# Recurrence in groups of one, one, two, two and two sequences beside the local streams, the input in three transfers, activation tables put in after planning

## Chip, cores and metric

One core of a Trainium2 chip runs the whole program. The metric is the device time in microseconds (us) of one launch; lower is better. PE is the matrix engine, DVE the vector engine, ACT the scalar engine with its function tables, POOL the general engine, and SP a sequencer that issues transfers.

## What is computed

Eight sequences of 256 tokens with 128 channels pass through eight layers, each followed by `layernorm(x + layer(x))`. Only the first three matter here.

```python
# layer 1: a gated linear recurrence (RG-LRU)
gate_x = sigmoid(block_diag_linear(x, ig_w, ig_b))
gate_a = sigmoid(block_diag_linear(x, ag_w, ag_b))
log_a = -8.0 * gate_a * softplus(a_param)
a, a2 = exp(log_a), exp(2.0 * log_a)
normed_x = x * gate_x * sqrt(clip(1.0 - a2, 1e-07))
p = cumprod(a, axis=1)
p_prefix = clip(concatenate([ones, p[:, :-1]], axis=1), 1e-07)
h = p_prefix * cumsum(normed_x / p_prefix, axis=1)
x = layernorm(x + h)
# layer 2: two blocks of local attention (window 64, 8 heads of 64) with a GELU feed-forward net
# layer 3: a Mamba block: gates, causal convolution, 16 states per channel scanned over time
# layers 4 to 8: a mixture of 32 experts (top 1), two attention blocks with 16 heads,
# a mixture of 8 experts (top 2) with a shared expert, typed attention, a ternary linear layer
```

Each sequence is independent in the first three layers, so layer 1 of one sequence can run beside layer 2 or 3 of another.

## The kernel before

The residual stream lies by channel: 128 partitions by 2048 columns, 256 columns for a sequence (`S`). Stages are traced one after another: `rglru`, `local_mamba`, `moe1`, `chunked`, `moe2`, `typed`.

**Recurrence.** `rglru_group(b0, tiles, work)` does four sequences at once in four tiles of 128 x 1024 (`gx`, `ga`, `sh`, `pp`). Two matmuls with `wg` for each pair of sequences give the gates (tile `gate`), ACT takes the sigmoids (L1013), two Exp (L1017, L1018), a Ln and an Exp (L1025, L1026). DVE does products, the running products and sums as scans (L1021, L1033) and a reciprocal (L1028). A layernorm per sequence ends it (L893 to L918): a matmul with `centre`, Square, a matmul with `mean`, Ln, Exp, a product into `x_rglru`. `rglru` runs it for sequences 0 to 3 and lets nothing else be traced meanwhile; sequences 4 to 7 are one more group inside `local_mamba`.

**Streams.** In `local_mamba`, `interleave` traces up to four generators `one_sequence(b)` at a time, each the two local blocks of a sequence, with a lag of 24 of its units; a finished sequence goes on to `mamba_sequence`, of which two are live. The group of sequences 4 to 7 is an extra generator. A local block starts with a shift of its input (tile `h`, L1062 to L1064), then matmuls `qk` and `vps` with `w_local`, transposes `qkt`, scores `sc`, maxima `nm`, exponentials `e` on ACT (L1146), transposes `pt`, outputs `o`, and a feed-forward net with GELU (`ge`, L1194). Before the first block, `w_local` is scaled by a layernorm weight and its bias is folded through small matmuls (`b1`, L1368, L1369). A Mamba sequence hands 33 rows to DRAM (`xs`, L1254), reads them back spread over the partitions (`bc`, L1262), and scans on DVE (`hs`, L1297 to L1300).

**Order.** After all stages are traced, `_Order` plans a list schedule over the instructions, with a cost per form (`LENGTHS`: time of occupation and time to the result, ns), a price for leaving PE's or ACT's present mode (`STAY`), and an offset per tile and stage added to the traced priority (`BIAS`). `impose` then makes each engine keep that order: no instruction overtakes another on its engine, and SP issues transfers in the planned order too. A transfer on SP also waits for the one issued eight before it, whose semaphore it takes over.

**Transfers.** `x_in` is one transfer of 1 MB. Two transfers clear the DRAM buffers `places` from a zeroed tile, 1.28 MB each. `w_local` comes in two of 1.56 MB.

**Activation tables.** ACT holds one set of functions at a time; a load (ACT_TABLE_LOAD in the profile, about 1283 ns) changes it. Where a function of the wrong set follows, the compiler puts a load in. The set with both Exp and Ln is asked for by hand: `exp_ln` adds a load in the traced program at set places (after sigmoids, GELU, Silu), bound to the instruction before it by `keep`, and the planner carries these loads along as instructions of set 1. One more load, for Silu, stands at the end of `route1`.

Of the kernel before, what the change touches and what calls it, by code (L numbers as in the profile page):

```python
# [23 lines left out]
P = 128  # L24
# [285 lines left out]
class _Order:  # L310
# [12 lines left out]
    STAY = dict(PE=70, ACT=310)  # L323
    BIAS = {
        "ACT  1": 495, "ACT  3": -495, "ACT d 2": -1445, "ACT e 4": -700, "ACT e 6": 370, "ACT fh 4": -30, "ACT four 4": 630, "ACT four 5": -345,
        "ACT ge 2": 385, "ACT got 3": 50, "ACT got 5": 590, "ACT k 2": -275, "ACT kp 4": -40, "ACT lakq 2": -75, "ACT lavp 2": -95, "ACT lg 2": 620,
        "ACT lnrs 1": 225, "ACT lnrs 2": -280, "ACT lnsq 2": 40, "ACT ot 6": 75, "ACT ptsb 2": -740, "ACT qsq 2": -5, "ACT r 2": -70, "ACT rg 1": -590,
        "ACT rg 2": -320, "ACT rn 2": 55, "ACT rs 4": -50, "ACT rs 6": -25, "ACT s 6": -190, "ACT savp 2": -5, "ACT sg 3": 560, "ACT sh 5": -250,
        "ACT spl 1": -410, "ACT spt 1": -15, "ACT st 6": 460, "ACT v 2": 25, "ACT xc 2": -2725, "ACT xchunked 2": -400, "ACT xchunked 4": -390,
        "ACT xs 2": 10, "ACT xsq 4": -660, "DVE ab 4": 720, "DVE bt 3": -1225, "DVE bt 5": 190, "DVE centre 0": -205, "DVE d 2": -10,  # L330
        "DVE decaypart 4": -240, "DVE e 2": 50, "DVE four 5": 105, "DVE fs 4": 10, "DVE gate 2": -345, "DVE gate 5": -320, "DVE get 2": 180, "DVE get 4": 5,
        "DVE get 5": 850, "DVE got 4": -40, "DVE h 2": 5, "DVE h 5": -525, "DVE hs 2": 5, "DVE k 5": -680, "DVE lares 2": -200, "DVE lg 4": 665,
        "DVE nm 2": -135, "DVE nm 6": -95, "DVE oh 2": -285, "DVE oh 4": 2440, "DVE oh 5": -180, "DVE ptsb 2": 20, "DVE ptsb 6": -250, "DVE put 2": 190,
        "DVE put 4": 480, "DVE q 5": 470, "DVE q 6": 785, "DVE r 2": -120, "DVE rc 2": -270, "DVE rc 4": 175, "DVE route 2": -345, "DVE s 2": 20,
        "DVE s 5": -95, "DVE s 6": 1585, "DVE sares 2": 30, "DVE sel 4": -50, "DVE sg 3": -250, "DVE sm 4": 365, "DVE spt 1": 810, "DVE st 6": 150,
        "DVE sum 2": -705, "DVE t 5": 400, "DVE th 4": 650, "DVE u 2": 255, "DVE vec 2": 50, "DVE we 4": -30, "DVE wlocal 2": 1325, "DVE xc 2": -1830,
        "DVE xla 4": -580, "DVE xlf 4": 75, "DVE xlocal 2": -860, "DVE xmoe 6": 10, "DVE xpf 4": -10, "DVE xrglru 2": 205, "DVE xsa 4": 485, "DVE ys 3": 100,
        "DVE z 4": -190, "PE a 2": 50, "PE acc 5": 10, "PE b 2": 30, "PE bt 3": 1010, "PE bt 5": -580, "PE cum 2": 80, "PE cum 4": -1270, "PE fold 2": 105,
        "PE g 2": -700, "PE gate 1": -345, "PE gate 2": 345, "PE hps 4": -15, "PE kps 4": 95, "PE lg 2": 205, "PE lin 6": -1140, "PE ln 1": 355,
        "PE ln 2": -45, "PE o 6": -910, "PE out 4": -35, "PE pg 5": -20, "PE proj 5": 100, "PE proj 6": -570, "PE ps 4": -455, "PE pt 2": -25,  # L340
        "PE pt 4": -125, "PE pu 3": 2550, "PE pu 5": -720, "PE py 3": 740, "PE qkt 2": -1425, "PE raw 2": -1360, "PE rows 2": 585, "PE sc 2": -60,
        "PE sc 4": 30, "PE sc 6": -1215, "PE v 5": 470, "PE v 6": -20, "PE vps 2": 1025, "PE vps 4": -10, "PE wo 2": 60, "PE wo 6": -855, "PE wout 2": -95,
        "PE xps 2": -790, "PE y 2": 20, "PE z 2": 40, "PE zt 4": -20, "POOL biasrows 3": -595, "POOL e 4": 415, "POOL e 6": -305, "POOL got 5": 490,
        "POOL km 5": 665, "POOL mean 0": 635, "POOL one 0": 395, "POOL places 2": -70, "POOL places 5": -240, "POOL q 5": 50, "POOL q 6": -325,
        "POOL rest 4": -990, "POOL rg 1": -25, "POOL rows 4": 85, "POOL ss 2": -20, "POOL t 2": 595, "POOL u 2": 110, "POOL zero 0": -35,
        "POOL zeros 1": -385, "SP bc 2": 200, "SP cst 3": -455, "SP got 3": 535, "SP got 5": 505, "SP outdram 6": 275, "SP places 1": 1460,
        "SP rottable 0": 45, "SP routetables 0": 495, "SP rows 4": -370, "SP scales 2": 40, "SP vec 0": -1475, "SP wattn 2": 15, "SP wmoe 2": -150,
        "SP wmoe 4": -150, "SP wmoe 5": -100, "SP xs 2": -660,
    }
    LENGTHS = {  # L350
        "ACT  LoadActFuncSet  ": (1178, 1283), "ACT d Ln 128x512 128x512": (544, 649), "ACT da Exp 128x255 128x255": (403, 508),
        "ACT e Abs 128x256 128x256": (460, 565), "ACT e Exp 128x128 128x128": (422, 527), "ACT e Exp 128x256 128x256": (460, 565),
        "ACT e Exp 128x512 128x512": (526, 631), "ACT four Exp 128x2 128x2": (98, 203), "ACT got DMACopy 128x512 128x512": (451, 3502),
        "ACT h TensorCopy 64x255 64x255": (295, 400), "ACT k TensorCopy 128x512 128x512": (484, 589), "ACT lnrs Exp 128x256 128x256": (317, 422),
        "ACT lnsq Square 128x256 128x256": (278, 383), "ACT ot TensorCopy 128x512 128x512": (490, 595), "ACT qsq Square 128x512 128x512": (498, 603),
        "ACT r Relu 128x256 128x256": (462, 567), "ACT rg Exp 128x1020 128x1020": (1039, 1144), "ACT rg Ln 128x1024 128x1024": (949, 1054),
        "ACT rn Exp 128x16 128x16": (111, 216), "ACT rn Ln 128x16 128x16": (116, 221), "ACT rs Exp 128x2 128x2": (97, 202),
        "ACT rs Ln 128x2 128x2": (98, 203), "ACT sh Silu 128x512 128x512": (492, 597), "ACT xc Identity 128x256 128x256": (465, 570),
        "ACT xc Silu 128x512 128x512": (524, 629), "ACT xchunked TensorCopy 128x256 128x256": (260, 365), "ACT xmoe Identity 128x256 128x256": (404, 509),
        "ACT xs TensorCopy 33x256 33x256": (255, 360), "ACT xsq Square 128x128 128x128": (296, 401), "DVE biaspart TensorCopy 96x256 96x256": (198, 283),  # L360
        "DVE decay TensorScalarPtr 128x512 128x512": (516, 601), "DVE decaypart TensorCopy 128x512 128x512": (334, 419),
        "DVE four TensorScalarPtr 128x4 128x4": (74, 159), "DVE ge TensorScalarPtr 128x256 128x256": (384, 469),
        "DVE ge TensorScalarPtr 85x256 85x256": (368, 453), "DVE h TensorTensor 128x256 128x256": (317, 402),
        "DVE hs TensorScalarPtr 128x1024 128x1024": (2191, 2276), "DVE hs TensorTensor 128x1024 128x1024": (1123, 1208),
        "DVE mv BNStatsAggregate 128x2 128x6": (85, 170), "DVE nm TensorTensor 128x8 128x8": (67, 152), "DVE ptsb TensorCopy 128x512 128x512": (594, 679),
        "DVE rc Reciprocal 128x16 128x16": (158, 243), "DVE rc Reciprocal 128x4 128x4": (83, 168), "DVE rc Reciprocal 128x8 128x8": (109, 194),
        "DVE rg TensorScalarPtr 128x256 128x256": (580, 664), "DVE rottable TensorScalarPtr 128x256 128x256": (260, 345),
        "DVE s TensorScalarPtr 128x128 128x128": (253, 338), "DVE s TensorTensor 128x256 128x256": (324, 409), "DVE st BNStats 128x6 128x128": (197, 282),
        "DVE sum TensorReduce 128x32 128x448": (736, 821), "DVE t TensorScalarPtr 128x256 128x256": (385, 470),
        "DVE t TensorTensor 128x512 128x512": (595, 680), "DVE vec TensorTensor 128x1 128x1": (60, 145), "DVE vec TensorTensor 85x1 85x1": (59, 144),  # L370
        "DVE vs TensorCopy 128x512 128x512": (594, 679), "DVE wlocal TensorScalarPtr 128x682 128x682": (483, 568),
        "DVE x TensorScalarPtr 128x256 128x256": (369, 454), "DVE xc TensorScalarPtr 128x254 128x254": (384, 469),
        "DVE xla TensorScalarPtr 128x256 128x256": (429, 514), "DVE xlocal TensorTensor 128x256 128x256": (310, 395),
        "DVE xpf TensorScalarPtr 128x256 128x256": (577, 662), "DVE z TensorScalarPtr 128x128 128x128": (292, 377),
# [62 lines left out]
    def group(self, i):  # L437
# [5 lines left out]
        if e == "ACT":  # L443
            return 1 if op == "LoadActFuncSet" else self.SETS.get(str(x.func).split(".")[-1]) if op == "Activation" else None
        return None

    def change(self, i):
        x, e, op = self.ops[i]
        if e == "ACT":
            return 0.0 if op == "LoadActFuncSet" else self.TABLE  # L450
# [120 lines left out]
    def length(self, i):  # L571
# [20 lines left out]
        if e == "ACT":  # L592
            if op == "LoadActFuncSet":
                return float(self.TABLE), float(self.TABLE)
# [1805 lines left out]
```

## Time and profile before

| | us |
|---|---|
| median of 8 runs | 1673.44 |
| lowest, highest | 1671.38, 1680.12 |
| the profiled execution | 1670.69 |
| its span from first to last instruction | 1668.6 |
| busy: PE | 1429.4 (86%) |
| busy: DVE | 1138.4 (68%) |
| busy: ACT | 975.3 (58%) |
| busy: POOL | 580.1 (35%) |

The mean granted clock of PE is 0.951 of full speed. Busy shares are means over stages with different limits: which wait matters is read stage by stage. In a row of the profile, `out<-in` are the program's tile names, `xN` the count, and the bracket after a row tells how long the engine was idle before it and what ended that.

### The profile page before, as it was taken

The numbers are of one execution on the slowest core, as the hardware profiler recorded it, in microseconds if no ns is written. First come the engines' busy times: TensorE is split into PE (matmuls) and PEld (weight loads), VectorE is DVE, ScalarE is ACT, GpSimd is POOL, SyncE is SP. The second block draws the span as 40 slices with busy tenths as digits, with TensorE's granted clock in tenths as the row PEclk, the third lists the DMA queues.
The fourth block names the chain that finished last, engine by engine and source line by source line (L and its number), as shares of the span: only waits on it lengthen the run. The fifth ranks groups of instructions, "written<-read, shape, count | busy, mean of one in ns | idle before, by whom it ended". The sixth has DMA issues, their size and how long they took to land.

```text
span 1668.6 us, 28693 instructions
## 1 busy us (share of the span) xinstructions
PE 1429.4 (86%) x10858; PEld 927.3 (56%) x10858; DVE 1138.4 (68%) x2182; ACT 975.3 (58%) x2661; POOL 580.1 (35%) x535
## 2 busy tenths in 40 slices
PE   2588897989797878677579999999997999999996
PEld 1345564545454544334367777677674775566664
DVE  5754579888989898689445566565545333588885
ACT  3777887777878779545125554545443222465654
POOL 1244452626263423200421122211214005657563
PEclk7899999999999998889789999999997999999998
DMA  5000012121212112156330000000102121000000
GB/s 196 1 1 1 1 40 64 40 64 40 64 40 64 52 51 90 52 177 214 122 115 2 8 11 11 11 7 6 44 5 68 47 81 37 15 5 4 8 5 10
DMA packets 45113, 77.97 MB, mean 47 GB/s; under 512 B 5580, under 2 KB 21988, under 8 KB 43824
## 3 DMA queue, kind: packets, MB, share of 16 engines
q1 hardware_dynamic: 39648, 70.02, 13.5%
q0 software_dynamic: 3216, 5.07, 1.1%
q8 instruction: 85, 1.39, 0.3%
q10 hardware_dynamic: 2112, 1.05, 0.2%
q14 instruction: 52, 0.43, 0.1%
HBM read 66.87 MB, written 10.76 MB: 47 GB/s over the span
## 4 chain that ended last, share of the span: by engine, by line
PE 50%; DVE 24%; ACT 10%; issue 8%; POOL 5%; DMA 2%; SPq 0%; ACTq 0%; DVEq 0%; POOLq 0%
PE vps L863 7%; PE kps L863 6%; PE sc L863 5%; DVE hs L1299 4%; PE out L863 4%; DVE hs L1300 3%; PE pg L863 3%; PE pu L863 3%; PE pt L974 3%; DVE hs L1297 2%; PE o L863 2%; ACT e L1146 2%; PE py L863 2%; PE hps L863 2%; PE acc L863 1%
## 5 line engine op out<-in xcount | busy, mean ns | idle before, releaser
L863 PE MATMUL y<-hs,ident 128*128 128x512 f32 x256 | 141.3, 667 | 30.4 <-DVE hs L1300 30.3
L1151 POOL TENSOR_TENSOR e<-e,rc 128x1024 f32<-128x1024 f32 x32 | 80.5, 2516 | 227.7 <-DVE rc L1150 227.1
L1299 DVE TENSOR_TENSOR_SCAN hs<-da,hs 128x1024 f32<-128x1024 f32 x64 | 154.1, 2409 | 0.2
L2250 ACT ACTIVATE e<-sc,nm 128x128 f32<-128x128 f32 (+1 forms) x256 | 104.9, 426 | 65.7 <-DVE nm L2245 58.9
L974 PE MATMUL pt<-ident,e 128*128 128x128 f32 x768 | 118.5, 280 | 18.0 <-POOL e L1151 12.1
L1295 ACT ACTIVATE da<-d,na 128x255 f32<-128x255 f32 x256 | 110.5, 507 | 22.2 <-DVE hs L1299 19.9
L1146 ACT ACTIVATE e<-sc,nm,rn 128x128 f32<-128x128 f32 x256 | 114.6, 469 | 10.5 <-DVE nm L1141 10.0
L974 PEld LDWEIGHTS pt<-ident,e 128*128 128x128 f32 x768 | 88.1, 142 | 56.7 <-issue 20.3
L2253 POOL TENSOR_TENSOR e<-e,rc 128x1024 f32<-128x1024 f32 x48 | 91.0, 1896 | 67.1 <-DVE rc L2252 67.0
L1829 POOL TENSOR_TENSOR e<-e,rc 128x512 f32<-128x512 f32 x32 | 33.8, 1057 | 224.3 <-DVE rc L1828 195.4
L1098 POOL TENSOR_TENSOR t<-t,t 128x512 f32<-128x512 f32 x64 | 84.0, 1316 | 59.9 <-DVE t L1085 55.8
L1804 ACT COPY kp<-kps 128x512 f32<-128x512 f32 x128 | 74.7, 584 | 48.5 <-PE kps L863 47.8
L1651 POOL DMA_INDIRECT got<-ybuf,get x48 | 45.6, 951 | 159.8 <-DMA ybuf<-ys 87.6
L863 PEld LDWEIGHTS y<-hs,ident 128*128 128x128 f32 x256 | 49.0, 209 | 78.4 <-DVE hs L1300 46.2
L1297 DVE TENSOR_TENSOR hs<-u,bc 128x1024 f32<-128x1024 f32 x64 | 87.2, 1378 | 6.4 <-POOL u L1284 5.5
L1300 DVE TENSOR_TENSOR hs<-hs,bc 128x1024 f32<-128x1024 f32 x64 | 87.6, 1371 | 0.0
L976 DVE COPY ptsb<-pt 128x512 f32<-128x512 f32 x104 | 69.1, 679 | 18.1 <-PE pt L974 17.1
L863 PE MATMUL qk<-w_local,h 128*128 128x512 f32 x128 | 70.1, 635 | 13.3 <-DVE t L1085 6.4
L1840 ACT COPY vs<-vps 128x512 f32<-128x512 f32 x64 | 37.3, 584 | 67.6 <-PE vps L863 54.9
L2245 DVE TENSOR_REDUCE nm<-sc 128x4 f32<-128x1024 f32 (+1 forms) x48 | 58.3, 1215 | 16.8 <-PE sc L863 16.2
L976 ACT COPY ptsb<-pt 128x512 f32<-128x512 f32 x88 | 51.3, 583 | 31.4 <-PE pt L974 30.7
L863 PE MATMUL vps<-sa_vp,x_lf 128*32 128x512 f32 x512 | 68.5, 594 | 0.0
(380 smaller groups left out, 3777.3 us busy)
## 6 DMA issues: line engine op xcount, KB each, us to landing
bc<-xs SPq DMA_DIRECT2D x128, 256.0 KB, 4.5
w_moe<-in_e_dram SPq DMA_DIRECT2D x16, 768.0 KB, 6.3
w_attn<-in_w_dram SPq DMA_DIRECT2D x4, 1024.0 KB
w_local<-in_w_dram SPq DMA_DIRECT2D x2, 1557.0 KB
places<-zeros SPq DMA_DIRECT2D x2, 1280.0 KB, 16.9
got<-places SPq DMA_DIRECT2D x6, 256.0 KB
ybuf<-ys SPq DMA_DIRECT2D x8, 160.0 KB, 2.2
x_in<-in_x_dram SPq DMA_DIRECT2D x1, 1024.0 KB
```

The lines of the kernel that those rows point to most:

```text
L863: return self.nc.tensor.matmul(out, lhsT, rhs, start=start, stop=stop)
L974: self.last = self.nc.tensor.transpose(pt[:, j * P : (j + 1) * P], src[:, j * P : (j + 1) * P], self.ident)
L976: copy(sb.rearrange("p a b -> p (a b)"), pt)
L1098: nc.gpsimd.tensor_add(t1, t1, t2)
L1146: nc.scalar.activation(e[:, j, g, :], scs[:, j, g, :], AF.Exp, bias=nm[:, j, g : g + 1], scale=rq[:, j, g : g + 1], accum_out=sm[:, j, g : ...
L1151: nc.gpsimd.tensor_tensor(e, e, rc.unsqueeze(3).to_broadcast([P, 2, 4, P]), ALU.mult)
L1295: nc.scalar.activation(da[:, n, c, 1:S], d[:, c, 1:S], AF.Exp, scale=na[:, i : i + 1])
L1297: nc.vector.tensor_tensor(hs, u.unsqueeze(1).to_broadcast(shp), bn, ALU.mult)
L1299: nc.vector.tensor_tensor_scan(line(hs), line(da), line(hs), 0.0, ALU.mult, ALU.add)
L1300: nc.vector.tensor_tensor(hs, hs, cn, ALU.mult)
L2250: nc.scalar.activation(e[:, i, :], sc[:, i, :], AF.Exp, bias=nm[:, i : i + 1], accum_out=sm[:, i : i + 1])
L2253: nc.gpsimd.tensor_tensor(e, e, rc.unsqueeze(2).to_broadcast([P, n, keys]), ALU.mult)
```

## The change

`rglru` keeps only the softplus of `a_param` and the clears of `places`. `rglru_group` takes a number of sequences `n`. Inside `local_mamba`, groups of sequences 0, 1, and 2 with 3 use the three `da` tiles of the Mamba scan and a `bc` tile as their four buffers; the group of sequence 0 is traced at once, the rest by an extra generator `recurrences` beside the streams. Sequences 4 with 5 and 6 with 7 are two more groups in the `hs` and `bc` tiles. `one_sequence(b)` waits in tracing until its recurrence has been traced.

```diff
-        nc.sync.dma_start(self.x, ins["x"])
+        nc.sync.dma_start(self.x[:, 0:S], ins["x"][:, 0:S])
...
+        nc.sync.dma_start(self.x[:, S : 4 * S], ins["x"][:, S : 4 * S])
...
-        for l in range(2):
-            nc.sync.dma_start(self.w0[:, l, :], ins["w0"][:, l * n : (l + 1) * n])
+        nc.sync.dma_start(self.w0[:, 0, :], ins["w0"][:, 0:n])
+        nc.sync.dma_start(self.x[:, 4 * S :], ins["x"][:, 4 * S :])
+        nc.sync.dma_start(self.w0[:, 1, :], ins["w0"][:, n : 2 * n])
...
-            tiles = [w.tile([P, 4, S], F32, name=f"rg{i}") for i in range(4)]
-            for _ in self.rglru_group(0, tiles, wk):
-                pass
...
-    def rglru_group(self, b0, tiles, work):
+    def rglru_group(self, b0, n, tiles, work):
...
-        for i in range(2):
-            bs = slice(2 * i, 2 * i + 2)
+        for i in range(0, n, 2):
+            bs = slice(i, min(i + 2, n))
...
+            four = [d.rearrange("p a b s -> p (a b) s") for d in das] + [scan.tile([P, 4, S], F32, tag="bc", name="rg", bufs=3)]
+            first = [self.rglru_group(b, n, [t[:, b : b + n] for t in four], work) for b, n in ((0, 1), (1, 1), (2, 2))]
+            for _ in first[0]:
+                pass
...
+            def recurrences():
+                yield from first[1]
+                yield 4.0
+                yield from first[2]
+                for d in das:
+                    nc.gpsimd.memset(d[:, :, :, 0:1], 0.0)
+                for i, gap in ((0, 16.0), (2, 10.0)):
+                    yield gap
+                    yield from self.rglru_group(4 + i, 2, [t[:, i : i + 2] for t in tiles], work)
...
             def one_sequence(b):
+                while self.recurred <= b:
+                    yield 1.0
...
-            interleave([one_sequence(b) for b in range(B)], 4, 24.0, then, 20.0, [self.rglru_group(4, tiles, work)])
+            interleave([one_sequence(b) for b in range(B)], 4, 24.0, then, 20.0, [recurrences()])
```

All calls of `exp_ln` go, with `keep` and the Silu load of `route1`. `impose` puts the loads of the Exp and Ln set in when the order stands:

```diff
         order, _ = self.plan()
+        ring, last = [], None
+        for i in order["ACT"]:
+            g = self.groups[i]
+            if g is not None:
+                if g == 1 != last:
+                    load = self.tc.nc.scalar.preload_act_table_set("natural_log_exp_and_others")
+                    self.ops.append((load.ins, "ACT", "LoadActFuncSet"))
+                    ring.append(len(self.ops) - 1)
+                last = g
+            ring.append(i)
+        order["ACT"] = ring
```

The planner's numbers are new throughout: `STAY` goes from PE 70 and ACT 310 to PE 140 and ACT 250, all of `BIAS` is replaced, and `LENGTHS` is renewed. Some of its entries:

```diff
+        "DVE da Reciprocal 128x256 128x256": (113, 198),
+        "DVE da Reciprocal 128x512 128x512": (113, 198),
+        "DVE rg Reciprocal 128x512 128x512": (113, 198),
+        "ACT rg Exp 128x510 128x510": (361, 466),
-        "POOL got DMACopy 128x128 2560x128": (949, 2493),
+        "POOL got DMACopy 128x128 2560x128": (1280, 2500),
+        "SP xin DMACopy 128x256 128x256": (350, 1815),
```

The order imposed is therefore a new one on every engine. On SP it begins with `w1`, `wg`, the two clears of `places`, `vec`, `rot_table`, `scales`, `route_tables`, then the three parts of `x_in` and the two of `w_local`; before it began with `vec`, `x_in`, `wg`, `w_local` (both), `w1`, `rot_table`, `scales`, `route_tables`, and the clears. The compiled program has 67 table loads where it had 73.

## The prediction

> **What bounds the kernel now.** I read the page, then the chain of waits from the start, then a table by stretch of time, then the timeline around single waits. Times are us of one profiled execution, which took 1670.69 with a span of 1668.6; the median of the runs shown is 1673.44, 2.75 above it.
>
> The chain first. Its columns are start, length, what was waited for.
>
> ```profile
> 1.67 5.99 DMA wg<-in_wg_dram
> 7.79 5.56 PE gate L863 x8
> ...
> 16.55 2.44 DVE rg L1021 x4
> ...
> 22.32 6.46 DVE rg L1028
> ...
> 36.32 6.65 PE ln L863 x16
> ...
> 44.38 0.40 ACT h L1064
> ```
>
> From 1.67 to 44.38 the chain is the recurrence of sequences 0 to 3, alone: gates, scan, a 6.46 us reciprocal, layernorms. The first matmul of a local stream follows:
>
> ```profile
> 18.28 4.62 POOL L1346 TENSOR_TENSOR rot<-rot_table,scales 128x256 f32<-128x256 f32 x4 [15.04 <-DMA scales<-in_qks_dram]
> 44.65 0.67 PE L863 MATMUL qk<-w_local,h 128*128 128x512 f32 x1 [0.76 <-DVE x_rglru L918]
> ```
>
> The stretches: after the engines' busy times come the granted clock, the DMA share and GB/s.
>
> ```profile
> core 0: us, PE busy (x) PEld busy (x) DVE busy (x) ACT busy (x) POOL busy (x), PEclk, DMA share, GB/s
> 28.50:44.65 16.15, 7.57 (x26) 6.08 (x27) 8.88 (x13) 4.74 (x14) 1.30 (x9) 0.57 0.00 0
> 44.65:100.00 55.35, 38.14 (x199) 20.23 (x200) 43.58 (x69) 40.42 (x91) 19.24 (x16) 0.85 0.00 1
> 100.00:233.00 133.00, 114.72 (x831) 71.32 (x832) 70.69 (x130) 105.02 (x299) 58.63 (x68) 1.00 0.00 1
> 233.00:749.00 516.00, 421.92 (x2284) 243.39 (x2283) 453.04 (x527) 392.23 (x988) 200.17 (x170) 0.95 0.23 67
> 819.00:1668.00 849.00, 799.28 (x7281) 559.57 (x7281) 494.40 (x1348) 389.03 (x1188) 276.98 (x238) 0.97 0.09 26
> ```
>
> Before 44.65 nothing is full. From 44.65 to 100 PE is busy 69%, although streams are ready: the second group of four holds DVE and ACT there. From 100 to 233, where the first Mamba sequence hands its rows to DRAM, PE is busy 86% and DVE only 53%. From 233 to 749 DVE leads with 88%. After 819 PE has 94%.
>
> **The head: 16 us less.** In the changed program SP issues w1, wg, the two clears of `places`, vec, the rotary table, scales, route tables, then x in three parts, then w_local in two. So the first part of x, though small, stands behind 4.07 MB: w1 0.45, wg 0.13, the mask 0.14, clears 2.62, vec 0.05, tables 0.54, itself 0.13. Before, scales stood behind 5.5 MB and landed at 18.28; the GB/s by 2 us add up to 3.76 MB at 12 us and 4.56 at 14, so queue order fits within 1 us. By that curve plus 0.8: vec lands at 11.9, the first x at 13.6, the halves of w_local at 20.7 and 24.9. The issue of the first half waits for the second clear, whose bytes are through at about 11; the queue still holds tables and x then, so it does not run dry.
>
> From vec, ACT has Abs 0.2, a table load 1.28, Exp, Ln, Relu and `na` about 1.0 with DVE between, the sigmoid load 1.28: 15.7. Two sigmoids (half of 0.69 plus start, 0.45 each): 16.6. Load 1.28, decay Exp 0.5: 18.4. DVE: scan 2.44/4 = 0.61, three scalar passes 0.35, reciprocal 6.54/4 = 1.64 and start, two products 0.4, scan 0.61, product and sum 0.4: 24.0. Layernorm of one sequence (Square 0.38, Ln 0.38, Exp 0.42, product 0.42, four matmul passes of 0.63 at the cold clock): 28.0. Shift 0.4: first qk at 28.6 instead of 44.65, so 16 us. The b1 matmuls wait for the second half of w_local, 24.9, and lie under that.
>
> **What comes back: 8 us.** Three quarters of the first group's work now lies beside the streams. PE: gates 5.54 minus two half ones, 4.2, and 3/4 of 6.65, in all 9.2 at a cold clock, 5.5 at full; I take 7. ACT: 3/4 of 11.9 (four sigmoids 2.8, four Exp and Ln 4.4, twelve layernorm steps 4.7) is 8.9; smaller groups cost more starts (a 1020-wide Exp 1.15, a 255-wide one 0.51), in all some 2.1; loads ahead of the first Mamba hand-over go from 22 to 24, 2.6. DVE: 17, and about 3 for more starts; from 100 to 233 it idles 62. Up to the first xps matmul, PE has 667 matmuls instead of 661 in program order, so Mamba starts after the same work. PE bounds the rate there: 7 / 0.86 = 8. The bounds are 0 (PE idles 17 from 44.65 to 100) and 33 (second rival). DVE behind is what could be late next.
>
> **Table loads.** 73 loads become 67: two more ahead of Mamba, already counted, and eight fewer behind, 8 x 1.28 = 10.3 of ACT. Most of these were loads of two sets in a row. ACT is busy 76% from 233 to 749 but has 10% of the chain, so the gain lies between 10% of 10.3, 1, and 76%, 8; I take 3, nearer the chain. The row of a switch:
>
> ```profile
> 108.65 2.64 ACT e L1146 x12
> 111.30 1.28 ACT L1194
> 112.60 0.85 ACT ge L1194 x2
> ```
>
> No gap stands on either side: a switch costs 1.28 here. The Trainium skill (ScalarE: Activation LUTs, What ACT_TABLE_LOAD costs) adds a drain and gives about 2.66 for each switch; by that the eight would free an estimated 21 of ACT, and with the same share the gain would be 6. The row decides.
>
> The Silu load ahead of the first mixture was placed early and now stands right before the first expert's activation `sg`; ACT idled 2.15 there behind PE (826.79), so it costs nothing, and 1.28 without that cover. The three `da` memsets (0.21 together) move on POOL behind the group of sequences 2 and 3, whose tiles they clear; the first Mamba scan, some 100 us later, is the only one to wait for them: nothing.
>
> **Three transfers.** Two more issues of 0.42 on SP, behind nothing that ACT or PE await: nothing. Small pieces did not slow the queue: 407 to 410 GB/s from 18 to 22 us, with clears and tables in flight. A rule speaks against this part: the Trainium skill (DMA: Bandwidth & Descriptors, Bandwidth) says to batch DMAs to 1 MiB or more for 75% of peak. By it, with its fixed 2.0 us for each of two more transfers paid in the open, an estimate of the gain would be 4 smaller. The transfers here stand in a queue, and I leave it at the row.
>
> **Order elsewhere.** The planner's costs and offsets all change, so every engine's order does. The instructions behind 819 are the same and PE is 94% busy there; I put 0, with 6 either way.
>
> Sum: -16 + 8 - 3 = -11. Span 1657.6, profiled time 1659.7, median 1673.44 - 11 = 1662.4. I say 1662.
>
> **Rivals.**
>
> *All of it is kept.* Pieces of 1 or 2 sequences fit idle slots: PE idles 17 and ACT 15 from 44.65 to 100, and the long reciprocal there no longer stalls everyone. Then 16 for the head and 8 for the loads: -24, 1649. Against: PE is 86% busy later, so moved work must be paid somewhere.
>
> *Each group stalls the streams: slower.* From 55 to 90 PE was busy 19 of 35 us, 11 under its 86%, while one group went through ACT and DVE in fixed order. Four groups now lie beside streams; at 11 each that is 44 instead of 11, 33 more, against 16 and 3: +14, 1687. For it: the diff's costs let a 512-wide reciprocal take 0.198, while the row says 6.54/2 = 3.3, and 0.198 for 256 where it is 1.64; that is 12 us of DVE time which the fixed order does not know of, with softmax maxima queued behind. Against: by sequences, not groups, it is 11 x 7/4 = 19, only 8 more than before. It decides from 19 us of new stall.
>
> *Nothing is left.* DVE bounds from 233 on and the Mamba cadence (hand-overs 85.6, 84.5 and 84 apart at first) does not care what came earlier: the moved DVE work of 20 us then returns the head's 16, and the loads' 3: about 1673.
>
> *It does not do what it says:* were x really late, behind slower clears (their 2.62 MB take 6.7 us at 390 GB/s, 12 at the 216 of an early slice), the head gains 11, and the sum is -6: 1667. It is inside the forecast.
>
> **Chances.** Forecast, between -4 and -20: 0.60. All kept or more: 0.11. Nothing left, within 0.2% or 3.3 us, about what a measurement of this kernel can tell from no change: 0.09. Stalls: 0.20. Faster 0.71, same 0.09, slower 0.20. The range 1648 to 1678 goes from all kept to a third of the way into the stalls.
>
> **What would show it.** In the profile after: the first qk at 28 to 30; clears landing ahead of x; the first Mamba hand-over at 222 to 227; 67 loads; from 819's counterpart on, 849 plus or minus 6. Wrong would be a first qk later than 36, a hand-over later than 233, or PE under 65% between the first qk and 100 us.

## The result, and the profile after

The changed kernel took 1681.13 us (median of 15 runs, 1678.2 to 1683.76) beside 1675.43 for the kernel before (42 runs): a ratio of 1.0035, 95% interval [1.0027, 1.0044]. It is slower by about 6, where the forecast was 11 faster. The profiled execution took 1679.41 with a span of 1677.6, 9.0 above the span before. Ten of the eighteen kernels run later fell on slower occasions, on which the kernel before takes 1695 instead of 1675 (the expectations call them a slower chip, but the record gives one chip number, 6, to occasions of both kinds); ratios are always to the kernel before on the same occasion.

The chain of waits of the changed kernel from the start (start, length, what was waited for):

```profile
3.04 1.19 SPq L810
...
4.26 1.38 SPq L813
...
8.24 8.65 DMA x_in<-in_x_dram
...
16.94 2.09 PE gate L877 x4
...
22.73 1.66 DVE da L1025
...
28.11 1.36 PE b L877 x8
...
30.53 0.52 PE b L877 x4
...
31.61 1.30 PE b L877 x6
32.91 1.06 PE gate L877 x2
33.97 2.56 PE qk L877 x3
```

The recurrence of four sequences before the first local stream has become that of one: its reciprocal takes 1.66 on the chain instead of 6.46. But the chain now begins with SP: the six issues behind the two clears take 1.19 to 1.44 each, and x lands only at 16.9. Just ahead of the first qk, PE does the bias matmuls `b` and gates of the next group. The timeline of the changed kernel shows what this does to ACT and PE:

```profile
13.39 0.20 ACT L1044 ACTIVATE sp_e<-vec 128x1 f32<-128x1 f32 x1 [11.37 <-DMA vec<-in_vec_dram]
...
16.98 0.23 ACT L1345 ACTIVATE na<-vec 128x32 f32<-128x32 f32 x1 [0.98 <-DMA x_in<-in_x_dram]
17.22 1.28 ACT L1011 ACT_TABLE_LOAD   x1
18.52 0.47 ACT L1011 ACTIVATE da<-gate,vec 128x256 f32<-128x256 f32 x1
...
33.76 2.77 PE L877 MATMUL qk<-w_local,h 128*128 128x512 f32 x3
```

`na` reads only `vec`, and the table load and the sigmoids stand behind it. Its row names x, which landed at the same time, but `na` needs nothing of x; what it follows, here as in e7 below, is the end of the softplus on DVE, `c`, at 16.81:

```profile
16.67 0.14 DVE L987 TENSOR_SCALAR c<-sp_l 128x1 f32<-128x1 f32 x1
```

That softplus could start only when `vec` was there, at 13.39. The first qk came at 33.76 instead of 44.65: 10.9 of the 16 that were forecast. The stretches (columns as in the prediction: busy times, then granted clock, DMA share, GB/s):

```profile
33.76:100.00 66.24, 46.83 (x232) 25.83 (x231) 40.85 (x70) 44.26 (x114) 21.28 (x25) 0.85 0.00 1
100.00:247.40 147.40, 123.56 (x815) 74.01 (x813) 95.32 (x157) 115.14 (x309) 58.88 (x66) 0.93 0.00 1
247.40:754.50 507.10, 425.35 (x2295) 243.97 (x2294) 450.03 (x525) 379.36 (x974) 205.08 (x168) 0.95 0.23 69
821.60:1281.20 459.60, 435.95 (x4803) 319.43 (x4803) 253.75 (x797) 214.47 (x505) 97.70 (x108) 0.98 0.08 23
1281.20:1677.00 395.80, 365.24 (x2479) 241.72 (x2478) 238.34 (x552) 175.90 (x685) 179.06 (x130) 0.97 0.10 29
```

From 100 to the first Mamba hand-over PE has a granted clock of 0.93, where it had 1.00, and DVE 95 us of work where it had 71. The hand-over comes at 247.4 instead of 233.0; the eighth at 754.5 instead of 749.2; the first mixture begins at 821.6 instead of 819.4. Behind that the instructions are the same, but the stretch to the first read of `rows_chunked` takes 459.6 instead of 452.3; the rest, 396, is unchanged. So in this pair 2 of the 9 arose before the mixture and 7 behind it; in the pair of repeats below (e6, e5) it is 7 and 4.

The runs on which the rest of this text rests, by their profiles: first qk, start of the 200th and of the 1000th matmul, first Mamba hand-over, start of the first mixture, from there to the end, and the ratio from the timed runs. An asterisk marks the slower occasions.

| kernel | qk | 200th | 1000th | hand-over | mixture | to the end | ratio |
|---|---|---|---|---|---|---|---|
| before | 44.7 | 97.4 | 222.5 | 233.0 | 819.4 | 849.2 | 1 |
| before, again (e6) | 45.4 | 97.8 | 223.4 | 234.0 | 820.7 | 849.6 | |
| changed | 33.8 | 86.5 | 233.6 | 247.4 | 821.6 | 856.0 | 1.0035 |
| changed, again (e5) | 34.0 | 87.6 | 237.1 | 250.9 | 827.8 | 853.7 | 1.0026 |
| changed, again (e13) | 33.8 | 86.9 | 236.3 | 250.1 | 824.0 | 853.3 | 1.0053 |
| clears last (e4)* | 44.4 | 96.4 | 249.9 | 263.6 | 837.9 | 868.4 | 1.0091 |
| clears last, `na` free (e7) | 28.0 | 81.0 | 230.0 | 243.8 | 820.9 | 853.9 | 0.9980 |
| reciprocals on ACT (e8) | 34.2 | 85.9 | 234.9 | 248.7 | 823.6 | 853.4 | 0.9998 |
| all three (e14) | 28.0 | 77.3 | 223.5 | 237.3 | 811.0 | 847.7 | 0.9957 |
| all three (e12)* | 28.1 | 78.3 | 222.7 | 236.5 | 816.2 | 868.6 | 0.9930 |
| changed, old order behind (e1)* | 33.5 | 86.6 | 235.9 | 249.8 | 823.7 | 872.1 | 1.0002 |
| changed, old order behind (e18)* | 34.0 | 87.4 | 236.9 | 250.8 | 827.6 | 868.9 | 1.0002 |
| changed without 1 to 3 (e10)* | 33.7 | 75.4 | 233.2 | 245.2 | 820.6 | 862.7 | |
| changed without 4 to 7 (e15) | 33.9 | 87.4 | 223.4 | 235.4 | 814.0 | 853.4 | |
| before without 4 to 7 (e17)* | 44.6 | 87.4 | 215.5 | 224.3 | 810.7 | 871.2 | |

Up to the mixture one kernel agrees with itself within about 6 from run to run; so smaller differences there show nothing by themselves. At the 200th matmul the changed kernel's profiles agree within 1.1, at the 1000th within 3.5. Where the values of a run differ, its ratio is left out.

### The profile page after: what moved, and what is told of

Same layout as the page of the kernel before. It is cut to its first block, busy times and chain, and to the rows that moved or that the text cites. A ratio compares the mean times of both kernels' runs of the same rounds, so it can differ in the third digit from the quotient of the medians.

```text
span 1677.6 us, 28721 instructions
## 1 busy us (share of the span) xinstructions
PE 1447.2 (86%) x10862; PEld 935.3 (56%) x10862; DVE 1141.4 (68%) x2209; ACT 970.2 (58%) x2669; POOL 587.1 (35%) x538
## 3 DMA queue, kind: packets, MB, share of 16 engines
q1 hardware_dynamic: 39936, 70.02, 13.4%
## 4 chain that ended last, share of the span: by engine, by line
PE 53%; DVE 24%; ACT 11%; issue 6%; POOL 4%; DMA 2%; SPq 0%; ACTq 0%; DVEq 0%; POOLq 0%
PE vps L877 7%; PE sc L877 6%; PE kps L877 6%; DVE hs L1296 4%; PE out L877 4%; PE pt L974 3%; PE pg L877 3%; PE pu L877 3%; PE o L877 3%; DVE hs L1297 3%; ACT e L1144 2%; DVE hs L1294 2%; PE py L877 2%; PE y L877 2%; PE hps L877 2%
## 5 line engine op out<-in xcount | busy, mean ns | idle before, releaser
L974 PE MATMUL pt<-ident,e 128*128 128x128 f32 x768 | 114.4, 280 | 18.9 <-ACT ptsb L976 6.8
L1096 POOL TENSOR_TENSOR t<-t,t 128x512 f32<-128x512 f32 x64 | 86.9, 1358 | 73.5 <-DVE t L1083 71.3
L1657 POOL DMA_INDIRECT got<-ybuf,get x48 | 45.8, 955 | 164.7 <-DMA ybuf<-ys 87.4
L1834 POOL TENSOR_TENSOR e<-e,rc 128x512 f32<-128x512 f32 x32 | 33.7, 1054 | 196.4 <-DVE rc L1833 106.7
L976 DVE COPY ptsb<-pt 128x512 f32<-128x512 f32 x104 | 68.9, 681 | 19.9 <-PE o L877 10.9
L1297 DVE TENSOR_TENSOR hs<-hs,bc 128x1024 f32<-128x1024 f32 x64 | 82.0, 1287 | 0.0
L877 PE MATMUL vps<-sa_vp,x_lf 128*32 128x512 f32 x512 | 75.2, 594 | 0.0
L877 PE MATMUL vps<-la_vp,x_moe 128*32 128x512 f32 x512 | 70.6, 594 | 0.1
```

The costliest lines, as they stand in the source:

```text
L877: return self.nc.tensor.matmul(out, lhsT, rhs, start=start, stop=stop)
L974: self.last = self.nc.tensor.transpose(pt[:, j * P : (j + 1) * P], src[:, j * P : (j + 1) * P], self.ident)
L976: copy(sb.rearrange("p a b -> p (a b)"), pt)
L1096: nc.gpsimd.tensor_add(t1, t1, t2)
L1297: nc.vector.tensor_tensor(hs, hs, cn, ALU.mult)
```

## The experiments

The theory at first: the recurrence groups stall the streams beside them, by work that the planner took for short (S), and the order behind the mixture is worse in itself (O). The rivals: the Mamba stretch gives back what comes earlier or later (C), and the head's missing 5 are the loss (H).

**The head.** e4 changes one offset (an entry of a long line), so that the clears are issued last:

```diff
-"SP places 1": -230
+"SP places 1": 4000
```

> One offset is changed, so that SP issues the two clears of places after w_local instead of ahead of vec and x; the other engines' orders stay but for some 1 per cent of their rows. vec should land at about 4 to 5 instead of 11.9 to 13, the first x at about 7, w_local at 15 and 19, and the first qk come at 25 to 28 instead of 33.76. Theory H (the head that was forecast 5 too early is part of the loss, each us of it counts): end 6 to 8 earlier, 1673 to 1675. Theory C: the end moves by 2 at most, 1679 to 1681.

1.0091 [1.0078, 1.0104]: slower instead of faster. x was there early (its gate matmul ran at 10.85), and yet the first qk came at 44.4. The timeline of that run names the reason:

```profile
26.95 0.23 ACT L1345 ACTIVATE na<-vec 128x32 f32<-128x32 f32 x1 [18.23 <-DMA places<-zeros]
27.20 1.28 ACT L1011 ACT_TABLE_LOAD   x1
```

`na` lies in the room of `zeros`, from which the clears are written, and may not be written before they have been read; ACT works in order, so the sigmoids wait too. Neither theory had this wait. In the changed kernel itself it cost nothing: there SP issued the first half of `w_local` at 12.62, an issue that waits for the second clear, so both clears were through before `na` could start. The run still weighs the head. e1 below has the changed kernel's order up to the mixture and ran beside e4; its first qk came at 33.5 and its mixture began at 823.7. In e4 the qk came 11 later and the mixture 14 later. (The end cannot be compared in this way, because the changed kernel was not run on a slower occasion.) e7 takes the room away from `na` and keeps the clears last; PE, DVE and ACT keep the changed kernel's order to the instruction:

```diff
-            zero = w.tile([P, 512], F32, name="zeros")
+            zero = self.y[:, T - 512 : T]
...
-"SP places 1": -230
+"SP places 1": 4000
```

> The changed kernel with the zeros, from which the clears of places are written, in the last quarter of x_rglru instead of a tile of their own whose room na and the da tiles take over; and the clears issued after w_local. PE, DVE and ACT keep the changed kernel's order to the instruction. The first sigmoid no longer waits for the clears: x was there at 10.9 in the run with the clears last, so the first sigmoid should start at about 11 to 12 instead of 18.5 and the first qk come at 26 to 29 instead of 33.8. Theory H (each us of the head counts at the end, as the 10.9 later first qk of the clears-last run cost 9.4): 5 to 7 earlier than the changed kernel, 1674 to 1676. Theory C (the streams give the head back): within 2 of it.

0.998 [0.9971, 0.9989], beside 1.0026 for the changed kernel run with it (e5): 0.0046, or 7.7, from a head 6 shorter, a little more than theory H had. The timeline of this run:

```profile
8.92 0.23 ACT L1345 ACTIVATE na<-vec 128x32 f32<-128x32 f32 x1 [0.54 <-DVE c L987]
9.17 1.28 ACT L1011 ACT_TABLE_LOAD   x1
12.40 0.47 ACT L1011 ACTIVATE da<-gate,vec 128x256 f32<-128x256 f32 x1 [1.95 <-PE gate L877]
```

Theory H holds in both directions for the changed kernel, and theory C is refuted.

**The long work beside the streams.** e2 and e3 keep the order and take away DVE's long reciprocals, or ACT's loads around the gates, for sequences 1 to 7 (the planner's entries that go with it are not shown):

```diff
-        nc.vector.reciprocal(sh, pp)
+        (nc.vector.tensor_copy if b0 else nc.vector.reciprocal)(sh, pp)
```

> Leaves out the reciprocal of the recurrence for sequences 1 to 7: a copy of the same shape stands in its place, planned at the same cost, so every engine's order is that of the changed kernel. It takes one wait of 1.75 and three of 3.35 (11.8 in all) off DVE and puts four copies of some 0.2 to 0.35 there, 10.6 less. Theory S (DVE's long reciprocals, planned at 0.198, stall the streams): the loss of 13 between 103 and 123 us and of 9 between 150 and 175 shrinks by 3 each or more, the first Mamba hand-over comes at 236 to 241 instead of 247.4, and the end 7 to 10 earlier, 1671 to 1674. Theory C (the Mamba stretch is bound by its own work and gives back what comes earlier): the hand-over moves, the end by 3 at most, 1678 to 1681.

```diff
-                nc.scalar.activation(flat(dst[:, bs]), ps, AF.Sigmoid, bias=self.v(bias))
+                nc.scalar.activation(flat(dst[:, bs]), ps, AF.Exp if b0 else AF.Sigmoid, bias=self.v(bias))
```

> Takes Exp in place of Sigmoid in the gates of sequences 1 to 7, planned as Sigmoid, so that every engine's order stays and only the table loads around those gates are gone: 10 loads of 1.28, 12.8 of ACT. Theory S (the switches of table set lie on the path of each group while streams wait in a fixed order): hand-over 5 to 10 earlier than 247.4, end 5 to 8 earlier, 1673 to 1676. Theory C: end within 3, 1678 to 1681.

The end is no measure here, since other values run through everything behind. Beside e1, which has the same front and ran with them (hand-over 249.8, mixture 823.7), e2 hands over at 241.0 and begins the mixture at 818.5: 8.8 and 5.2 earlier. e3 does so at 246.5 and 822.8: 3.3 and 0.9. So the reciprocals weigh at the hand-over, and ten table loads hardly do. e8 keeps the values and replaces the reciprocals; the order is planned anew with true costs:

```diff
-        nc.vector.reciprocal(sh, pp)
+        nc.scalar.activation(sh, pp, AF.Ln)
+        nc.scalar.activation(sh, sh, AF.Exp, scale=-1.0)
```

> The changed kernel with the five long reciprocals (1.75 twice, 3.35 three times, 13.5 of DVE) done as Exp(-Ln) on ACT: ten more instructions of 0.42 to 0.62, 5.4 of ACT, planned with their true costs; the result is the same. Theory S (DVE's reciprocals are the stall): first Mamba hand-over at 236 to 242 instead of 247.4, end 5 to 8 earlier than the changed kernel, 1673 to 1676. Theory A (ACT with its table loads is the stall): end the same or up to 4 later, 1681 to 1685.

0.9998 [0.9989, 1.0007], 0.0028 or 4.7 below the changed kernel, so theory A fails. But theory S had more at the end, 5 to 8, and a hand-over at 236 to 242; it came at 248.7, where the changed kernel's three profiles have 247.4 to 250.9. So the gain did not show where theory S looked for it, and whether it comes from the reciprocals or from the new order is not separated. e16 makes the same edit in the kernel before:

> The kernel before with its two reciprocals of 6.46 as Exp(-Ln) on ACT (four more instructions of about 1.06). Theory R (the reciprocals are no part of what the change costs): the one in the head alone saves 4, both 5 to 9, ratio 0.995 to 0.997. Theory S (they cost only where streams run beside them, which is the change's doing): 2 to 4 from the head's one, ratio 0.998 to 0.999.

0.9994 [0.9982, 1.0005], no measurable gain. The first qk came at 41.0, some 4 earlier, but the mixture began at 822.2. Theory R fails: there 12.9 of DVE and 4 of the head were worth nothing that could be measured (theory S's 0.998 to 0.999 lies within the interval). A shorter head thus paid in the changed kernel and not in this one, whose order was planned anew around it.

How the reciprocal stands in the way shows the chain of the changed kernel where the group of sequences 4 and 5 passes:

```profile
100.01 1.28 ACT L1011
...
102.59 1.28 ACT L761
...
104.64 1.27 DVE rg L1018 x2
...
106.90 3.26 DVE rg L1025
110.16 0.54 DVE ptsb L976
...
118.20 2.63 DVE rg L1033
```

The copy `ptsb` of a local stream, and PE's `o` behind it, stand behind a reciprocal that the planner took for 0.198.

**Groups.** e11 has one late group instead of two (the costs of its wider forms, as in the kernel before, are not shown):

```diff
-                for i, gap in ((0, 16.0), (2, 10.0)):
-                    yield gap
-                    yield from self.rglru_group(4 + i, 2, [t[:, i : i + 2] for t in tiles], work)
+                yield 16.0
+                yield from self.rglru_group(4, 4, tiles, work)
```

> The changed kernel with sequences 4 to 7 in one group of four, as in the kernel before, instead of two groups of two; the costs of the 1020- and 1024-wide forms are those of before. Theory G (each group stalls the streams once, by 11): one group fewer, 5 to 10 faster than the changed kernel, 1671 to 1676. Theory L (what stalls is the length of the work, 6.5 in one reciprocal instead of twice 3.35): the same or up to 5 slower, 1680 to 1686.

1.0035 [1.0023, 1.0048], on a slower occasion; hand-over 260.3, mixture 834.3. One group fewer brings nothing, and the front is later by 6 to 13. Theory G is refuted; theory L, that the length of the work counts and not the number of groups, stands, though a new order came with the edit. e10 leaves sequences 1 to 3 out of the recurrence, e15 sequences 4 to 7 by the same lines under `if b0 > 3`, and e17 does as e15 in the kernel before:

```diff
+        if b0 in (1, 2):
+            for b in range(n):
+                self.layernorm(work, x[:, b], y[:, b * S : (b + 1) * S])
+                self.recurred = b0 + b + 1
+                yield 2.0 * part
+            return
```

> The changed kernel without the recurrence of sequences 1 to 3 (their x is only normalised; gates, scans, reciprocal left out): what the change moved beside the streams, taken away. The values differ from there on, so it is read up to the first mixture, not behind. Forecast (what was moved costs 8): the first mixture begins 8 earlier than in the changed kernel on the same chip, 814 to 816 where that has 822 to 824. Theory S (the moved groups cost more than the lead of 11 that they bought): 11 to 16 earlier. Theory B (moved work fills gaps and the late groups 4 to 7 cost the time): 0 to 5 earlier.

> The changed kernel without the recurrence of sequences 4 to 7 (their x is only normalised). Read up to the first mixture, since the values differ from there on. Theory P (the lead of 11 at 100 us was borrowed from the groups that the change put off until 100 to 180 us): first Mamba hand-over 12 to 20 earlier than the changed kernel in the same call, the first mixture 8 to 13 earlier. Theory F (these groups fill gaps): hand-over 5 to 8, mixture 3 to 5 earlier, as without sequences 1 to 3.

> The kernel before without the recurrence of sequences 4 to 7 (their x is only normalised); read up to the first mixture, as the values differ behind. Theory P (that group was nearly free at its old place, where PE idles anyway, and moving it is the loss): the first mixture begins 1 to 5 earlier than the 819.4 and 820.7 of the kernel before. Rival (it costs the same 10 wherever it stands): 9 to 12 earlier, 808 to 811; then the loss lies elsewhere.

Without sequences 1 to 3, PE has done 200 matmuls at 75.4 instead of 86.5: the moved groups cost 11 there. At 1000 matmuls they cost 0.4, at the mixture 3 (beside e1's 823.7), both within what runs differ by. Without sequences 4 to 7 the changed kernel's 1000th matmul comes 12.9 earlier than in e13, run beside it, the hand-over 14.7 and the mixture 10.0. Two rows of the stretches, of e13 and of e15:

```profile
100.00:125.00 25.00, 17.95 (x91) 10.93 (x92) 18.94 (x27) 17.47 (x40) 5.99 (x7) 0.79 0.00 1
```

```profile
100.00:125.00 25.00, 20.57 (x120) 11.47 (x120) 14.80 (x28) 19.58 (x56) 10.17 (x12) 1.00 0.00 1
```

PE does 91 matmuls instead of 120 while a late group passes, and its granted clock falls to 0.79. That looked like the whole loss, but e17 refutes it as such: in the kernel before, the same four sequences cost 9 to 10 as well (mixture 810.7 beside 819.4 and 820.7; 200th matmul 87.4 beside 97.4). The kernel before pays this before 97, the changed one after 100. So its lead of 10.9 at the 200th matmul was owed: without the late groups both kernels are there at 87.4. By the hand-over these groups cost 9 to 10 in the kernel before (224.3 beside 233.0 and 234.0) and 14.7 in the changed one, by the mixture about the same in both.

**Order.** e1 gives the changed kernel the old numbers from the first mixture on; e18 repeats it:

```diff
-        self.rank = [x.bass_priority + self.BIAS.get(f"{k} {g}", 0) for k, g, (x, _, _) in zip(self.key, stage, self.ops)]
+        self.rank = [x.bass_priority + (self.BIAS2 if g > 2 else self.BIAS).get(f"{k} {g}", 0) for k, g, (x, _, _) in zip(self.key, stage, self.ops)]
```

with `LENGTHS` and `STAY` alike. The order behind the mixture is then that of the kernel before, instruction by instruction.

> The changed kernel with the numbers of the kernel before (offsets, stay, lengths) for the first mixture and everything behind it; the order up to 819.4 of the kernel before (821.6 of the changed one) is that of the changed kernel, the order behind it that of the kernel before, instruction by instruction. Theory O (the changed numbers alone make the rear slower): from the first gather of the mixture to the end it takes 849 again instead of 856, so the time falls by 7, to 1674, ratio 0.999 to the kernel before. Theory S (the groups beside the streams cost the time, and the rear differs because the front hands over differently): the rear stays at 856, time 1681, ratio 1.0035.

> The changed kernel with the old numbers, and so the old order, behind the first mixture, once more. Theory O: where the kernel before takes 1675, the stretch from the mixture to the end takes 847 to 850 instead of 853 to 856, and the ratio is 0.002 to 0.004 under the 1.0035 of the changed kernel. Theory K (nothing in whole runs): 1.003 to 1.005.

1.0002 [0.9993, 1.0011] and 1.0002 [0.9992, 1.0011]. Both have the order of the kernel before behind the mixture and are compared with it on the same occasion, so they weigh the changed front alone: it is worth nothing, within 2 us, where the forecast was 11. Whether the order behind the mixture is the rest cannot be read from them, because both fell on slower occasions, where the changed kernel itself was never run. There the stretch from the mixture to the end takes 872.1, 868.9 and 868.6 with the old order (e1, e18, e12), and 868.4 and 863.2 with the new one in e4 and e11 (860 to 864 in e2, e3 and e10, which carry other values): no gain from the old order. On the faster occasions it takes 847.7 to 849.6 with the old order (before, e6, e14, e16) and 853.3 to 856.0 with the new one (changed, e5, e7, e8, e13, e15), so 4 to 8 are lost to order there. This is theory O on one kind of occasion and theory K between the two. Repeats of the two kernels gave the rows for it:

> The changed kernel itself once more, beside the kernel before on the chip of the runs that follow, since the chip of the first experiments is 1.2 per cent slower than that of the two profiles shown. Theory O (order behind 819 as such is worth 7): ratio 1.0035 again, and the chunked stage takes 7 longer than in the kernel before. Theory K (the 7 depends on the chip's clock): the two chunked stages differ by less than 3 here, and the ratio is near 1.000.

> The kernel before itself, for a profile of it on the same chip: by both theories a ratio of 1.000; its chunked stage (from the first gather of the first mixture to the first read of rows_chunked) 452 if that length belongs to its order, 462 to 466 if it belongs to the chip.

> The changed kernel, on the chip of the three runs that follow. Theory O (the order behind the first mixture costs 5 to 7 wherever it runs): 1.003 again on any chip. Theory K (that cost depends on the chip): on a chip on which the kernel before takes 1695, the ratio is 0.996 to 0.999, and on one where it takes 1675 it is 1.003.

The old order itself took 452.8 up to `rows_chunked` in e6, the new one 460.1 and 459.7 in e5 and e13. What differs inside is how the matmuls on 32 rows overlap. Kernel before, from 819.4 to 1271.7: the row of the stretch (columns as above), then two of the costliest groups (count, the time in which at least one runs, the mean in ns):

```profile
819.40:1271.70 452.30, 429.07 (x4803) 320.03 (x4803) 256.98 (x798) 214.02 (x506) 97.76 (x108) 0.97 0.08 24
L863 PE MATMUL vps<-sa_vp,x_lf 128*32 128x512 f32 x512 | 68.5, 594 | 0.0
L863 PE MATMUL out<-vs,ptsb 128*32 128x128 f32 x1024 | 42.6, 274 | 0.0
```

The same groups of the changed kernel, from 821.6 to 1281.2:

```profile
L877 PE MATMUL vps<-sa_vp,x_lf 128*32 128x512 f32 x512 | 75.2, 594 | 0.0
L877 PE MATMUL out<-vs,ptsb 128*32 128x128 f32 x1024 | 53.3, 275 | 0.0
```

The single matmuls last the same; as many of them hold PE 7 and 11 longer, so fewer run side by side. PE's busy time as a whole grew by 6.9 (429.07 to 435.95), near the 7.3 by which the stretch grew.

e9 is the kernel before with its table loads put in after planning, and nothing else; the order is planned anew:

```diff
-        self.exp_ln(last)
...
         order, _ = self.plan()
+        ring, last = [], None
+        for i in order["ACT"]:
...
```

> The kernel before with one part of the change alone: its table loads are put in once the order is planned (10 loads fewer than before in this program), with the numbers of before; structure and transfers as before, the order replanned. Forecast's term (3 for eight loads behind the Mamba start, by ACT's place between 10 and 76 per cent of the path): 3 to 5 faster than the kernel before, ratio 0.997 to 0.998. Rival (the loads lie off the path; in the run without ten of them the first mixture began only 0.9 earlier): within 2 of before, 0.999 to 1.001.

1.0152 [1.0139, 1.0165]. Neither theory foresaw 25 lost by ten loads fewer. The hand-overs of the kernel before and of e9:

```profile
L1254 SPq DMA_DIRECT2D xs<-xs x8: 302/303/378, 233.0 to 749.2; - x8
```

```profile
L1259 SPq DMA_DIRECT2D xs<-xs x8: 303/303/378, 235.5 to 773.7; - x8
```

The first comes 2.5 later, the eighth 24.5. The edit only takes instructions away, so the order is what is left to have lost the time: the offsets were fitted to another set of instructions. The run tells nothing of the price of a load; it tells how much order alone is worth.

**All three taken away.** e12 and e14 join e7, e8 and the old order behind the mixture:

> The changed kernel with three things together: the zeros in x_rglru and the clears last (0.0046 of the time in its own run), the reciprocals on ACT (0.0028), and the order behind the first mixture of the kernel before (0.0029). If they add up: ratio to the kernel before 1.003 - 0.0103 = 0.993, 1663. If they hide one another in the Mamba stretch: 0.997, 1670.

> The kernel with the three things together once more, beside the changed kernel on one chip. If the three terms add up wherever it runs: 0.993 to the kernel before, and 0.010 below the changed kernel. If the order behind the mixture gains only on one kind of chip: 0.993 to before again, but only 0.004 to 0.007 below the changed kernel where before takes 1695.

0.993 [0.9915, 0.9944] on a slower occasion; 0.9957 [0.9942, 0.9972] beside 1.0053 [1.0036, 1.0069] for the changed kernel on a faster one. The difference of 0.0096 there is near the sum of the three, 0.0103, of which the 0.0029 for the order was taken across occasions. It beats both kernels.

## Why the prediction was wrong, point by point

**The head: 16 forecast, 10.9 found.** SP's order was as read, and the mechanism held in the main; the size was 5.2 too large. Of these, 2.8 arose up to the first sigmoid, at 18.5 instead of 15.7: `vec` was used at 13.4 instead of 11.9, and from there the softplus, `na` and the table load took 5.1 instead of 3.8. x was used at 16.9 instead of 13.6; by the 1.23 that e7 takes from the first gate matmul to the sigmoid, x alone would have held the sigmoid until about 18.2, an estimate. Bytes were counted, but the six issues behind the clears took 1.2 to 1.4 each instead of 0.42, so that the first part of x was issued only at 8.24, and the rate of the transfers fell from 409 GB/s between 8 and 10 us to 212 between 12 and 14, where the forecast had a queue that does not run dry. `vec` was issued early, at 3.04; why it came 1.5 late is open.

The other 2.3 arose between the first sigmoid and the first qk, 15.2 instead of 12.9: the `b` matmuls were to lie under the wait for the recurrence, but the chain has them between and behind the layernorm's matmuls. The room of `zeros` under `na` was not seen, but it counts only where the clears come last (e4). A head 6 shorter was worth 7.7 of the end (e7).

**What comes back: 8 forecast, all of the head's 10.9 found.** This is the step that failed. The sum priced the moved groups by PE's busy share, 7 / 0.86, and let half of the lead stand. They cost 11 at the 200th matmul (e10), as much as the head had gained, and the changed front as a whole is worth nothing at the end (1.0002, e1 and e18). The sum also put at nothing that the second group, which held the streams before 97, holds them again after 100: its 10 were paid at a new place, not saved, and the lead seen at the 200th matmul was this debt. The rest is not resolved: with the late groups left out of both, the changed kernel falls from level at the 200th matmul to 7.9 behind at the 1000th, and to 3.3 at the mixture, which is within what runs differ by. From 87.4 to the hand-over it has four layernorms more there (the late sequences', which the kernel before does earlier) and another order; what each of the two costs stays open.

**Table loads: 3 forecast.** Six loads went, as read (74 and 68 in the profiles, one more in each than the compiled program counts), and 1.28 without a gap is right (100.01 and 102.59 above), against the drain that the Trainium skill adds (ScalarE: Activation LUTs, What ACT_TABLE_LOAD costs). But ten loads around the gates were worth 0.9 at the mixture, within what runs differ by. For the loads behind the Mamba start the term is unproved.

**Three transfers, `da` memsets: 0.** The two further issues took 1.44 and 0.45 on SP instead of 0.42 each, with only `w_local` behind them. Nothing in the traces speaks against the term; no run took these parts alone.

**Silu load: 0 forecast.** The forecast hid it in the 2.15 for which ACT waits for PE ahead of `sg`. The changed kernel's timeline has the wait first and the load behind it, so `sg` is 1.28 later than it could be, and PE's next `pg` waits 0.81 for it; the kernel before has no such wait there. What it adds at the end was not measured alone.

```profile
828.95 1.28 ACT L1706 ACT_TABLE_LOAD   x1 [2.11 <-PE pg L877]
830.24 0.44 ACT L1706 ACTIVATE sg<-pg 128x320 f32<-128x320 f32 x1
...
830.73 1.12 PE L877 MATMUL pg<-bt,w_moe 128*128 128x80 f32 x8 [0.81 <-ACT sg L1706]
```

**Order elsewhere: 0, plus or minus 6.** It is a loss of 4 to 8 on the faster occasions, and with a front worth nothing (e1, e18) that would be all of the 6 by which the kernel got slower. That PE was 94% busy did not speak for 0: an order in which fewer matmuls overlap made PE busy 6.9 longer up to `rows_chunked`, and that stretch 7.3.

**The rivals.** The slower one, four stalls of 11, had the sign and the wrong mechanism: e11 refutes its count by groups, and by the mixture the late groups cost about 10 in both kernels (e15, e17) and the moved ones some 3 (e10), far from its 33 more. Its evidence, reciprocals planned at 0.198, stands on the chain at 106.90, and replacing them, with a new order, was worth 4.7 of the end (e8); the sum had left them out as hidden in DVE's idle time. The rival by which nothing is left is near to what the front did (1.0002), but it had no term for the order behind the mixture. The forecast's wrong signs, first qk after 36 and PE under 65%, did not come; a hand-over after 233 did.

## What to carry to other kernels

A head start counts only with the work that was put off to get it: compare two kernels at the same work done, the moved and the delayed parts included, before calling idle time a gap. When a change comes with new planner numbers, look for costs that are false (0.198 for 3.35), and give order a term of its own with a bound from a run; ten instructions fewer under ill-fitting offsets moved this program by 1.5%. Before moving a transfer, ask what tile takes over the room of its source.

## What the hardware showed

- An issue on SP took 0.42 to 0.43 for the eight transfers behind `w` in e4, where the clears come last, and 1.19 to 1.44 for the six right behind the two clears in the changed kernel. The size alone does not explain it: right behind the two halves of `w_local`, larger than the clears, the kernel before issued at 0.46 to 0.49. The same transfer in the changed kernel and in e4, by SP's timeline:

```profile
3.04 1.19 SPq L810 DMA_DIRECT2D vec<-in_vec_dram  x1
```

```profile
1.67 0.42 SPq L810 DMA_DIRECT2D vec<-in_vec_dram  x1
```

- A product of two tensors in SBUF on DVE took 2.63 instead of 0.68 beside a POOL product of 1.89 (timeline of the changed kernel, DVE, then POOL):

```profile
118.20 2.63 DVE L1033 TENSOR_TENSOR rg<-rg,x_in 128x512 f32<-128x512 f32 x1
...
118.39 1.89 POOL L1149 TENSOR_TENSOR e<-e,rc 128x1024 f32<-128x1024 f32 x1
```

DVE ended at 120.83, 0.55 after POOL: it seems to have stood still for all of POOL's instruction, although it had begun first. The Trainium skill says that the two contend (SBUF — State Buffer, Who interferes with whom): a DVE instruction with two SBUF inputs contends with a GpSimd instruction that reads SBUF.

- DVE's reciprocal took 3.35 for 512 elements per partition and 1.75 for 256; a product took 0.68 for 512 and 0.42 for 256.
- The same program took 1675 on some occasions and 1695 on others. Up to the mixture they agree; the old order behind it takes 848 to 850 on the one kind and 869 to 872 on the other, the new one 853 to 856 and 860 to 868. One trace of it: with the old order the 1024 `out` matmuls hold PE 42.6 on the faster occasions, and 47.4 to 48.1 in e1, e12, e17 and e18, with 4.2 to 4.7 of idle time before them for which the profile finds no wait ("issue"). The row of e1, from 823.7 to 1289.2:

```profile
L970 PE MATMUL out<-vs,ptsb 128*32 128x128 f32 x1024 | 47.9, 275 | 4.5 <-issue 4.4
```

Why is open, and the changed kernel's ratio on the slower occasions was not measured.
